# Layer 2's convolution stage of a four-layer kernel: how its strips, loads, stores and token passes are arranged

## The chip, the cores and the metric

The kernel runs on one core of a Trainium2 chip. TensorE (PE in the profile) multiplies matrices, VectorE (DVE), ScalarE (ACT) and GpSimd (POOL) do the element-wise work, and SyncE (SP) issues transfers. A transfer can also be issued from ACT's queue or POOL's. Each engine takes its own instructions strictly in order. The metric is the device time of one execution in microseconds, lower is better.

## The reference

Four layers are chained, each as x = x + layer(groupnorm(x)), on a tensor of 4 images, 384 channels and 64x64 positions in fp32. Layer 0 is an attention, layer 1 a convolution with an 8x8 Fourier filter, layer 3 a 7x7 convolution whose taps depend on the input. The change lies in layer 2, whose core is this:

```python
y3 = _bn(_dw(x, c3_w, 1), c3_g, c3_b)
y5 = _bn(_dw(x, c5_w, 2), c5_g, c5_b)
y1 = x * c1_w.reshape(1, -1, 1, 1) + c1_b.reshape(1, -1, 1, 1)
tok = _bn(kw[:, 0:1] * y3 + kw[:, 1:2] * y5 + y1, ar_g, ar_b)
```

`_dw` is a depthwise convolution (3x3 and 5x5), `_bn` a normalisation of each channel over images and positions, `kw` two weights per image from a small network. After it come a channel gate and a two-matrix network, `cm_w1` (384 to 768) and `cm_w2` (768 to 384).

## The kernel before

The phases run one after the other: `phase_a` (layers 0 and 1), `phase_b` (the convolution stage of layer 2), `phase_ef` (its two matrices), `phase_g` (layer 3). All four are written out as straight code. The framework puts each engine's instructions in an order near that of the program and adds the semaphores.

**Layer 1 of the last image** (image 3) has no attention beside it. It works in 8 bands of 8 rows. `band_out` (L1142) ends each band: two matmuls per output tile, an addition on DVE (L1152), statistics (L630), and a store of the result to DRAM as `x1` from POOL's queue (L1155).

**Strips.** `phase_b` computes the depthwise convolutions as matmuls. Its stationary operand is `z`, a tile of 128 channels in which each channel's image rows are laid out in pairs ("strips", made by TensorE transposes of the normalised x and copied out of PSUM with a scatter). For the first 128 channels, images 0 to 2 are put into `z` by `strips_of` while layer 1 of image 3 runs. Image 3's are made at the head of `phase_b` by `strips5` (L1316): four loads of x1 from DRAM, a normalisation on ACT (L1320), 32 transposes (L1325) and 8 copies to `z` (L1331 on ACT, L1329 on DVE).

**Units.** The 384 channels are worked in 12 units of 32 channels, with all 4 images in the 128 partitions. One unit has 16 steps of two channels each. In a step:

- `matrices53` (L1339) builds the band matrix of the step three steps ahead, from taps loaded on POOL's queue by `taps53` (L1337). Most even steps are built on DVE, odd ones on POOL (L1351).
- `conv53` (L1359) runs 12 matmuls (L1370) into a PSUM bank `conv_m` (4 buffers), two ACT copies into `d_o` (L1379, L1381), two DVE statistics (L1384). Every fourth step stores `d_o` (1 MB) to the DRAM tensor `d53[u]` from ACT's queue (L1386).

Three other streams are threaded through the steps as generators, a piece at a time:

- `unit_strips` (L1261) loads a unit's x1 (two tiles of 1 MB, 8 transfers each, L1272 on SP's queue, into 6 buffers `b_x`), normalises it in four parts (L1280, ACT) and, from unit 4 on, transposes it into `z` (L1294, L1301, L1299). Unit u+1 is processed during unit u.
- `conv_norms` (L1391) turns the finished unit's statistics into factors.
- `unit_tok` (L1427) works on unit u-1 during unit u. For each quarter of 1024 positions it loads 1 MB of convolution results, `c_d` (L1436, SP's queue, 3 buffers), then for each of two halves runs an ACT affine into the single PSUM buffer `tok_m` (L1444) and two DVE operations (L1449, L1451). Then comes an ACT square with a running sum (L1456), and a 512 KB store of the tokens from SP's queue (L1463). The square's output goes to the `c_d` tile, so that tile is free only when the square is done.

After the last unit its own `unit_tok` runs alone, then `tok_stats`, then a short serial chain of small normalisations at the start of `phase_ef`, whose first matmul is L1604. `phase_ef` loads `cm_w2_t` at its beginning, from ACT's queue (L334), although the second matrix is used only half of the phase later (L1658).

Of the kernel before, what the change touches and what calls it, by code (L numbers as in the profile page):

```python
# [281 lines left out]
class _Builder:  # L282
# [859 lines left out]
    def band_out(self, b, acc, h, st):  # L1142

        nc = self.nc
        x = self.block("xa_out", self.xa[b], h, "xo", 2)
        for o in range(NJ):
            m = self.pa("out_m1") if b == B - 1 else self.pm("out_m")
            nc.tensor.matmul(m, lhsT=self.w_out[:, 0, o * P : (o + 1) * P], rhs=acc[1], start=True, stop=False)
            nc.tensor.matmul(
                m, lhsT=self.w_out[64:P, 1, o * P : (o + 1) * P], rhs=acc[2][64:P], start=False, stop=True  # L1150
            )
            nc.vector.tensor_add(x[:, o], x[:, o], m)  # L1152
            yield 2.0
        self.stats(st, x, h)
        nc.gpsimd.dma_start(self.x1[b][:, :, h * 512 : (h + 1) * 512], x)  # L1155


# [3 lines left out]
    def open_strips(self, ctx):  # L1161

        pool = ctx.enter_context(self.tc.tile_pool(name="strips", bufs=1, side="right"))
        self.z_ = pool.tile([P, P * 136 + 4], F32, tag="z", name="z")
        self.z = self.z_[:, 0 : P * 132].rearrange("p (c k b) -> p c k b", k=33, b=B)
        self.nc.gpsimd.memset(self.z[:, :, 0], 0.0)
        self.nc.gpsimd.memset(self.z_[:, P * 132 : P * 132 + 4], 0.0)

    def phase_b(self):
# [5 lines left out]
        with ExitStack() as ctx:  # L1175
# [10 lines left out]
            self.taps53(0)  # L1186
            self.toep = {}
            for n in range(LEAD + 2):
                self.matrices53(n)
            for q in range(4):  # L1190
                x = self.bx_p.tile([P, 2048], F32, tag="x", name="in_x1")[:, 0:1024]
                self.strips5(0, B - 1, x, 8 * q, self.pm)
            self.units(cp)
            self.unit_x = [[] for _ in range(UNITS)]
            strips, behind = self.unit_strips(1), None
            next(strips)
            for u in range(UNITS):
                st = self.bt_p.tile([P, 2, 16, 6], F32, tag="st", name="st")
                tok = self.unit_tok(u - 1) if u else self.unit_strips(0)
                nets = iter(()) if u else self.nets(cp)  # L1200
                for n in range(16):
                    if u or n > 1:
                        self.matrices53(16 * u + n + LEAD)
                    self.conv53(u, n, st)
                    if n == 0 and u:
                        self.conv_norms(u - 1, behind)
                    if n % 2:
                        next(strips, None)
                    elif n or not u:
# [15 lines left out]
            self.tok_stats()  # L1225

# [34 lines left out]
    def unit_strips(self, u):  # L1261
# [22 lines left out]
        load(0)  # L1284
        norm(0)
# [73 lines left out]
    def conv53(self, u, n, st):  # L1359
# [6 lines left out]
        m = self.psum.tile([P, 512], F32, tag="c", name="conv_m", bufs=4)  # L1366
# [59 lines left out]

    def unit_tok(self, u):  # L1427

        nc = self.nc
        j, q = u // 4, u % 4  # L1430
        s, s0 = self.tok_s
        for i in range(4):
            sl = slice(i * 1024, (i + 1) * 1024)
            d = self.bc_p.tile([P, 8, 2, P], F32, tag="d", name="c_d")
            o = self.unit_x[u][i // 2][:, i % 2 * 1024 : i % 2 * 1024 + 1024]
            nc.sync.dma_start(  # L1436
                d.rearrange("p y v n -> p y (v n)"),
                self.d53[u][8 * i : 8 * i + 8].rearrange("y b c v n -> (b c) y (v n)"),
            )
            for h in range(2):  # L1440
                part = slice(h * 512, (h + 1) * 512)
                last = u == UNITS - 1
                m = self.psum.tile([P, 512], F32, tag="c" if last else "t", name="tok_m", bufs=4 if last else 1)
                nc.scalar.activation(  # L1444
                    m, o[:, part], AF.Identity, bias=s0, scale=self.vec("c1_w")[:, u : u + 1]
                )
                mv, ov = (t.rearrange("p (y n) -> p y n", n=P) for t in (m, o[:, part]))
# [6 lines left out]
                if h == 0:  # L1454
                    yield
            nc.scalar.activation(  # L1456
                d.rearrange("p y v n -> p (y v n)")[:, 0:1024],
                o,
                AF.Square,
                bias=self.about[:, u : u + 1],  # L1460
                accum_out=self.squares[:, u, i : i + 1],
            )
            nc.sync.dma_start(self.tok[u, :, :, sl].rearrange("b c n -> (b c) n"), o)  # L1463
            yield
# [59 lines left out]
    def phase_ef(self, strips):  # L1524
        tc, nc = self.tc, self.nc
        with ExitStack() as ctx:
            self.open_psum(ctx)
            cp = ctx.enter_context(tc.tile_pool(name="ef_const", bufs=1))
            w2 = self.weight(cp, "cm_w2_t")
# [50 lines left out]
            for b in range(B):  # L1580
                for i in range(4):
# [18 lines left out]
                    for o in range(6):  # L1600
# [13 lines left out]
                        if o % 2:  # L1614
# [11 lines left out]
                            )  # L1626
                    nc.gpsimd.dma_start(self.wx[b][:, :, blk], x)
# [501 lines left out]
```

## Time and profile before

| what | us |
|---|---|
| median of three runs | 4785.09 |
| the runs | 4772.37, 4785.09, 4792.93 |
| the profiled execution, its own time | 4780.85 |
| its span, first to last instruction | 4779.1 |
| `phase_b`'s first matmul of the convolution | 2452.7 |
| end of its last | 3005.8 |
| first matmul of `phase_ef` (L1604) | 3063.6 |

The page gives, for each engine, the time in which it was busy. Over the whole span that is PE 4377.5 us (92%), DVE 2846.8 (60%), ACT 1964.3 (41%) and POOL 832.4 (17%). Such shares are averages over stages with different limits. To read one stage one asks for the busy time of every engine in stretches of it, with the granted clock of TensorE, the busy share of the 16 transfer engines and the bytes per second. Times in these stretches count from the start of the span.

### The profile page before, as it was taken

The page shows a single profiled execution, that of the slowest core. Times are in us where ns is not written, and L with a number is a line of the kernel's source. Part 1 is how long each engine was busy: PE and PEld are TensorE (multiplying, and loading weights), DVE is VectorE, ACT ScalarE, POOL GpSimd, SP SyncE. Part 2 cuts the span into 40 slices and gives each one's busy share as a digit, 9 for nine tenths or more (in the row PEclk, how much of TensorE's full clock was granted, in tenths as well). Part 3 has the DMA queues.
Part 4 walks back from the last instruction along what each step waited for, and adds up shares of the span by engine and source line. Part 5 has one row for each costly group of instructions (what it writes and reads, how often), then busy time and mean ns, then how long its engine had stood idle before and what let it go on. Part 6 is the DMA issues. An engine that isn't in the chain of part 4 may idle for free. (4 is left out here: it accounts for less than half of the span.)

```text
span 4779.1 us, 49753 instructions
## 1 busy us (share of the span) xinstructions
PE 4377.5 (92%) x18445; PEld 2442.5 (51%) x18445; DVE 2846.8 (60%) x4647; ACT 1964.3 (41%) x2904; POOL 832.4 (17%) x779
## 2 busy tenths in 40 slices
PE   6999999999999999989978899599999999578889
PEld 2233444344443444434457788344444444578889
DVE  7766566645566355565867677655531111777788
ACT  4444444444444443435445566311123332764321
POOL 1000000000000000000035455000000000436665
PEclk9999999999999999999988899799999999688999
DMA  4301211121211111112249789776764333897787
GB/s 144 104 32 65 79 60 67 59 67 38 75 53 62 55 40 60 60 64 97 90 153 308 257 292 305 270 263 251 261 235 178 144 147 131 333 348 235 241 274 259
DMA packets 286592, 747.66 MB, mean 156 GB/s; under 512 B 22555, under 2 KB 123014, under 8 KB 274310
## 3 DMA queue, kind: packets, MB, share of 16 engines
q1 hardware_dynamic: 219832, 442.03, 28.8%
q0 software_dynamic: 40320, 179.59, 10.1%
q10 hardware_dynamic: 26190, 122.76, 6.5%
q8 instruction: 149, 2.44, 0.2%
q14 instruction: 101, 0.83, 0.1%
HBM read 442.04 MB, written 302.25 MB: 156 GB/s over the span
## 5 line engine op out<-in xcount | busy, mean ns | idle before, releaser
L819 ACT ACTIVATE probs<-sc_s 128x1024 f32<-128x1024 f32 x512 | 496.6, 1020 | 688.2 <-PE av L929 588.6
L929 PE MATMUL av<-probs,vt 128*128 128x512 f32 x1536 | 714.9, 602 | 0.0
L1128 DVE SCALAR_TENSOR_TENSOR acc<-band,vecs,acc 128x512 f32<-128x512 f32 x708 | 496.1, 745 | 44.9 <-POOL band L1089 39.7
L1658 PE MATMUL h_m<-f_h,cm_w_t 128*128 128x512 f32 x1152 | 497.1, 594 | 7.4 <-ACT f_h L1646 7.4
L1370 PE MATMUL conv_m<-toep,z 128*128 128x192 f32 (+1 forms) x2304 | 445.8, 355 | 9.2 <-DVE z L1299 9.2
L929 PEld LDWEIGHTS av<-probs,vt 128*128 128x128 f32 x1536 | 275.6, 191 | 338.1 <-issue 334.4
L1987 PE MATMUL conv_m<-toep,z 128*128 128x128 f32 x3072 | 396.4, 287 | 32.5 <-DVE toep L1974 20.6
L1370 PEld LDWEIGHTS conv_m<-toep,z 128*128 128x128 f32 x2304 | 409.6, 197 | 31.9 <-DVE z L1299 9.8
L1987 PEld LDWEIGHTS conv_m<-toep,z 128*128 128x128 f32 x3072 | 382.6, 204 | 34.8 <-issue 13.2
L1604 PE MATMUL h_s<-e_tok,cm_w_t 128*128 128x512 f32 x768 | 362.8, 595 | 4.2 <-DVE e_tok L1589 4.2
L1658 PEld LDWEIGHTS h_m<-f_h,cm_w_t 128*128 128x128 f32 x1152 | 219.7, 191 | 284.8 <-issue 274.7
L1666 DVE BATCH_NORM_STATS2 h_st<-f_h 128x6 f32<-128x512 f32 x96 | 66.4, 693 | 429.6 <-ACT f_h L1665 429.6
L811 PE MATMUL sc_s<-q,k 32*128 32x512 f32 x2048 | 306.6, 642 | 14.9 <-ACT probs L819 14.7
L1351 POOL TENSOR_TENSOR toep<-w,band 128x1280 f32<-128x1280 f32 x94 | 272.3, 2897 | 240.0 <-PE conv_m L1370 236.8
L1051 PE MATMUL t_m<-w_in_t,xb 128*128 128x384 f32 x768 | 279.2, 498 | 4.2 <-DVE coef L1068 4.0
L965 PE MATMUL proj_m<-xm,w_proj_t 128*128 128x512 f32 x576 | 271.8, 611 | 6.3 <-DVE xm L904 4.9
L1611 ACT COPY e_h<-h_s 128x1024 f32<-128x1024 f32 x96 | 97.2, 1013 | 399.6 <-PE h_s L1604 395.5
L1613 DVE BATCH_NORM_STATS2 h_st<-e_h 128x6 f32<-128x512 f32 x192 | 123.5, 685 | 207.9 <-ACT e_h L1611 207.9
L1604 PEld LDWEIGHTS h_s<-e_tok,cm_w_t 128*128 128x128 f32 x768 | 146.3, 191 | 188.0 <-issue 183.2
L1051 PEld LDWEIGHTS t_m<-w_in_t,xb 128*128 128x128 f32 x768 | 143.0, 192 | 142.1 <-issue 60.0
L972 DVE SCALAR_TENSOR_TENSOR x_res<-proj_m,bn_c,x_res 128x512 f32<-128x512 f32 x96 | 71.7, 747 | 236.4 <-PE proj_m L965 236.3
L1604 PE MATMUL h_s<-z,cm_w_t 128*128 128x512 f32 x384 | 196.1, 592 | 0.0
(426 smaller groups left out, 6371.6 us busy)
## 6 DMA issues: line engine op xcount, KB each, us to landing
d<-d_o ACTq DMA_DIRECT2D x48, 1024.0 KB
c_d<-d SPq DMA_DIRECT2D x48, 1024.0 KB
hid<-e_h ACTq DMA_DIRECT2D x16, 3072.0 KB
f_h<-hid SPq DMA_DIRECT2D x16, 3072.0 KB
x_in<-in_x SPq DMA_DIRECT2D x96, 256.0 KB
x_res<-in_x SPq DMA_DIRECT2D x32, 768.0 KB
xa<-x_res POOLq DMA_DIRECT2D x32, 768.0 KB, 3.9
xa_out<-xa SPq DMA_DIRECT2D x32, 768.0 KB
```

The costliest lines, as they stand in the source:

```text
L811: nc.tensor.matmul(s[:, g], lhsT=k4[32 * g : 32 * g + 32, c], rhs=q[i][32 * g : 32 * g + 32], start=True, stop=True,)
L819: nc.scalar.activation(p[:, h * 1024 : (h + 1) * 1024], s[:, 2 * h : 2 * h + 2].rearrange("p a b -> p (a b)"), AF.Exp, scale=0.25,)
L929: nc.tensor.matmul(av[0], lhsT=vt[:, 4 * c + v, :], rhs=p[:, v * 512 : (v + 1) * 512], start=c == 0 and v == 0, stop=c == 7 and v == 3,)
L965: nc.tensor.matmul(m, lhsT=self.w_proj[:, j, o * P : (o + 1) * P], rhs=xm[:, j], start=j == 0, stop=j == NJ - 1,)
L1051: nc.tensor.matmul(m[:, 0:C], lhsT=xb[:, j], rhs=self.w_in[:, j, :], start=j == 0, stop=j == NJ - 1,)
L1128: nc.vector.scalar_tensor_tensor(out, src(j, k), w, done, ALU.mult, ALU.add)
L1351: eng.tensor_tensor(t, self.w53[:, at : at + 160].rearrange("p (m n) -> p m n", n=8).unsqueeze(2).to_broadcast([P, 20, 8, 8]), band.rearra ...
L1370: nc.tensor.matmul(m[:, c * 256 + to : c * 256 + to + 64 * (k1 - k0)], lhsT=self.z_[:, at : at + P], rhs=t[:, 10 * c + k0 : 10 * c + k1].r ...
L1604: nc.tensor.matmul(s[:, v, :], lhsT=w1[:, j, o * P : (o + 1) * P], rhs=t[j][:, v * 512 : (v + 1) * 512], start=j == 0, stop=j == NJ - 1,)
L1613: nc.vector.bn_stats(st[:, o, 8 * b + 2 * i + v, :], h[:, o, v * 512 : (v + 1) * 512])
L1658: nc.tensor.matmul(m, lhsT=w2[:, o, j * P : (j + 1) * P], rhs=h[:, o, v * 512 : (v + 1) * 512], start=o == 0, stop=o == 5,)
L1987: nc.tensor.matmul(m[:, ch % 4 * P : (ch % 4 + 1) * P], lhsT=self.z_[:, at : at + P], rhs=t[:, 8 * c + 2 * i : 8 * c + 2 * i + 2].rearrang ...
```

## The change

In the order of the program:

1. Image 3's strips of the first 128 channels are transposed, not normalised, at the end of each band of layer 1 (`raw_strips`). At the head of `phase_b` the factors of the group norm are spread over the partitions (`strip_factors`, one matmul), and `z` is scaled in place (`scale_strips`): 8 channels on DVE, then 24 on DVE, then three times 32 on POOL at steps 3, 7 and 11 of unit 0. The loads, normalisations, transposes and copies of `strips5` for that image go.
2. The first taps are loaded when the strips' pool is opened, into a pool of their own with 2 buffers (3 before).
3. `units` and `nets` move behind the first convolution step. A unit's first x tile is asked for at step 11, and no longer at step 15, of two units earlier, and a `yield` parts that load from its normalisation.
4. The results of a finished unit are asked for at step 0 of the next (three tiles), and the fourth when the first tile's square is done. The last unit's four tiles use the `b_x` buffers.
5. `tok_m` has 2 buffers and `conv_m` 3. The square of a quarter, and its store, follow behind the next quarter's first affine (`square_and_store`), and the store is issued from ACT's queue. In the last unit, the tokens of the unit before are taken in larger portions.
6. `cm_w2_t` is loaded from POOL's queue after the second block of `phase_ef`.

```diff
@@ -1151,9 +1151,37 @@
+        if b == B - 1:
+            self.raw_strips(b, h, x[:, 0])
         self.stats(st, x, h)
...
+    def raw_strips(self, b, h, x):
+
+        m = self.pm("strip_m")
+        for k in range(4):
+            self.nc.tensor.transpose(m[:, k * P : (k + 1) * P], x[:, k * P : (k + 1) * P], self.ident)
+        self.nc.scalar.copy(self.z[:, :, 1 + 4 * h : 5 + 4 * h, b], m.rearrange("p (k c) -> p c k", c=P))
+
+    def strip_factors(self, b):
+
+        nc = self.nc
+        x = self.bx_p.tile([P, 2048], F32, tag="x", name="z_rep")
+        t, self.z_rep = (x[:, 256 * i : 256 * i + 256].rearrange("p (i c) -> p i c", i=2) for i in range(2))
+        for i, v in enumerate((self.r2, self.n2)):
+            nc.vector.tensor_scalar(t[:, i], self.ident, v[:, 0, b : b + 1], float(P), ALU.mult, ALU.mult)
+        m = self.pm("z_rep")[:, 0 : 2 * P]
+        nc.tensor.matmul(m, lhsT=self.mean128, rhs=t.rearrange("p i c -> p (i c)"), start=True, stop=True)
+        nc.vector.tensor_copy(self.z_rep, m.rearrange("p (i c) -> p i c", i=2))
+
+    def scale_strips(self, b, c0, n, eng):
+
+        at = slice(c0, c0 + n)
+        zv = self.z[:, at, 1:33, b]
+        of = lambda i: self.z_rep[:, i, at].unsqueeze(2).to_broadcast([P, n, 32])
+        eng.tensor_mul(zv, zv, of(0))
+        eng.tensor_add(zv, zv, of(1))
@@ -1165,6 +1193,9 @@
+        self.taps_s = ExitStack()
+        self.taps_p = self.taps_s.enter_context(self.tc.tile_pool(name="b_taps", bufs=2, side="right"))
+        self.taps53(0)
@@ -1183,46 +1214,62 @@
-            self.taps53(0)
             for n in range(LEAD + 2):
+                if n == 1:
+                    self.strip_factors(B - 1)
+                    self.scale_strips(B - 1, 0, 8, nc.vector)
+                if n == 3:
+                    self.scale_strips(B - 1, 8, 24, nc.vector)
                 self.matrices53(n)
-            for q in range(4):
-                x = self.bx_p.tile([P, 2048], F32, tag="x", name="in_x1")[:, 0:1024]
-                self.strips5(0, B - 1, x, 8 * q, self.pm)
-            self.units(cp)
             self.unit_x = [[] for _ in range(UNITS)]
-            strips, behind = self.unit_strips(1), None
-            next(strips)
+            first, strips, behind = self.unit_strips(0), self.unit_strips(1), None
+            next(first)
             for u in range(UNITS):
                 st = self.bt_p.tile([P, 2, 16, 6], F32, tag="st", name="st")
-                tok = self.unit_tok(u - 1) if u else self.unit_strips(0)
-                nets = iter(()) if u else self.nets(cp)
                 for n in range(16):
                     self.conv53(u, n, st)
+                    if n == 0 and not u:
+                        self.units(cp)
+                        nets = self.nets(cp)
+                        for _ in range(2):
+                            next(first)
+                    if n == 0 and u > 1:
+                        next(before, None)
                     if n == 0 and u:
+                        self.results = [self.load_results(u - 1, i) for i in range(3)]
                         self.conv_norms(u - 1, behind)
+                    if not u and n in (3, 7, 11):
+                        self.scale_strips(B - 1, 8 * n + 8, 32, nc.gpsimd)
                     if n % 2:
                         next(strips, None)
                     elif n or not u:
                         next(tok, None)
-                    if n == 15 and u:
+                    if u == UNITS - 1 and n or u and n == 15:
                         next(tok, None)
+                    if not u and n in (1, 3):
+                        next(strips)
...
                     if n % 3 == 2:
                         next(nets, None)
-                    if n == 15 and u + 2 < UNITS:
-                        strips = self.unit_strips(u + 2)
-                        next(strips)
-                behind = st
+                    if n in (11, 15) and u + 2 < UNITS:
+                        if n == 11:
+                            coming = self.unit_strips(u + 2)
+                        next(coming)
+                        if n == 15:
+                            strips = coming
+                behind, before = st, tok
+            self.results = [self.load_results(UNITS - 1, i, self.bx_p, "x") for i in range(4)]
             self.conv_norms(UNITS - 1, behind)
             for _ in self.unit_tok(UNITS - 1):
                 pass
             self.tok_stats()
+        self.taps_s.close()
@@ -1282,6 +1329,7 @@
             )
 
         load(0)
+        yield
         norm(0)
         yield
-            self.w53_ahead = self.bt_p.tile([P, 8 * 80], F32, tag="w53", name="w53", bufs=3)
+            self.w53_ahead = self.taps_p.tile([P, 8 * 80], F32, tag="w53", name="w53", bufs=2)
-        m = self.psum.tile([P, 512], F32, tag="c", name="conv_m", bufs=4)
+        m = self.psum.tile([P, 512], F32, tag="c", name="conv_m", bufs=3)
+    def load_results(self, u, i, pool=None, tag="d"):
+        pool = pool or self.bc_p
+        d = pool.tile([P, 2 * 8 * P], F32, tag=tag, name="c_d").rearrange("p (y v n) -> p y v n", v=2, n=P)
+        self.nc.sync.dma_start(
+            d.rearrange("p y v n -> p y (v n)"),
+            self.d53[u][8 * i : 8 * i + 8].rearrange("y b c v n -> (b c) y (v n)"),
+        )
+        return d
+
...
+        results, self.results = self.results, None
+        behind = None
         for i in range(4):
-            sl = slice(i * 1024, (i + 1) * 1024)
-            d = self.bc_p.tile([P, 8, 2, P], F32, tag="d", name="c_d")
+            d = results[i]
             o = self.unit_x[u][i // 2][:, i % 2 * 1024 : i % 2 * 1024 + 1024]
-            nc.sync.dma_start(
-                d.rearrange("p y v n -> p y (v n)"),
-                self.d53[u][8 * i : 8 * i + 8].rearrange("y b c v n -> (b c) y (v n)"),
-            )
             for h in range(2):
                 part = slice(h * 512, (h + 1) * 512)
-                last = u == UNITS - 1
-                m = self.psum.tile([P, 512], F32, tag="c" if last else "t", name="tok_m", bufs=4 if last else 1)
+                m = self.psum.tile([P, 512], F32, tag="t", name="tok_m", bufs=2)
                 nc.scalar.activation(
                     m, o[:, part], AF.Identity, bias=s0, scale=self.vec("c1_w")[:, u : u + 1]
                 )
+                if h == 0 and behind is not None:
+                    self.square_and_store(u, *behind)
+                    if len(results) == 3:
+                        results.append(self.load_results(u, 3))
                 mv, ov = (t.rearrange("p (y n) -> p y n", n=P) for t in (m, o[:, part]))
                 of = lambda v: d[:, 4 * h : 4 * h + 4, v]
                 nc.vector.scalar_tensor_tensor(mv, of(1), s[:, 1:2], mv, ALU.mult, ALU.add)
-                if h == 0:
-                    yield
...
-            nc.sync.dma_start(self.tok[u, :, :, sl].rearrange("b c n -> (b c) n"), o)
-            yield
+                yield
+            behind = i, d, o
+        self.square_and_store(u, *behind)
...
+    def square_and_store(self, u, i, d, o):
...
+        nc.scalar.dma_start(self.tok[u, :, :, i * 1024 : i * 1024 + 1024].rearrange("b c n -> (b c) n"), o)
@@ -1526,7 +1586,7 @@
-            w2 = self.weight(cp, "cm_w2_t")
+            w2 = cp.tile(list(self.ins["cm_w2_t"].shape), F32, tag="cm_w2_t", name="cm_w2_t")
...
+                    if b == 0 and i == 1:
+                        nc.gpsimd.dma_start(w2, self.ins["cm_w2_t"])
```

More of the change, by code (lines that the diff above doesn't have):

```diff
@@ L1185, in phase_b @@
             nc.gpsimd.memset(self.mean128, 1.0 / P)
-            self.taps53(0)
             self.toep = {}
             for n in range(LEAD + 2):
+                if n == 1:
[3 more added lines that the diff above has]
+                    self.scale_strips(B - 1, 8, 24, nc.vector)
                 self.matrices53(n)
-            for q in range(4):
-                x = self.bx_p.tile([P, 2048], F32, tag="x", name="in_x1")[:, 0:1024]
-                self.strips5(0, B - 1, x, 8 * q, self.pm)
-            self.units(cp)
             self.unit_x = [[] for _ in range(UNITS)]
-            strips, behind = self.unit_strips(1), None
-            next(strips)
+            first, strips, behind = self.unit_strips(0), self.unit_strips(1), None
+            next(first)
             for u in range(UNITS):
                 st = self.bt_p.tile([P, 2, 16, 6], F32, tag="st", name="st")
-                tok = self.unit_tok(u - 1) if u else self.unit_strips(0)
-                nets = iter(()) if u else self.nets(cp)
+                tok = self.unit_tok(u - 1) if u else first
                 for n in range(16):
@@ L1425, in conv_norms @@
         self.tok_s = s, s0
+    def load_results(self, u, i, pool=None, tag="d"):
[6 more added lines that the diff above has]
+        return d
     def unit_tok(self, u):
         nc = self.nc
-        j, q = u // 4, u % 4
         s, s0 = self.tok_s
+        results, self.results = self.results, None
+        behind = None
         for i in range(4):
-            sl = slice(i * 1024, (i + 1) * 1024)
-            d = self.bc_p.tile([P, 8, 2, P], F32, tag="d", name="c_d")
+            d = results[i]
             o = self.unit_x[u][i // 2][:, i % 2 * 1024 : i % 2 * 1024 + 1024]
-            nc.sync.dma_start(
-                d.rearrange("p y v n -> p y (v n)"),
-                self.d53[u][8 * i : 8 * i + 8].rearrange("y b c v n -> (b c) y (v n)"),
-            )
             for h in range(2):
                 part = slice(h * 512, (h + 1) * 512)
-                last = u == UNITS - 1
-                m = self.psum.tile([P, 512], F32, tag="c" if last else "t", name="tok_m", bufs=4 if last else 1)
+                m = self.psum.tile([P, 512], F32, tag="t", name="tok_m", bufs=2)
                 nc.scalar.activation(
@@ L1453, in unit_tok @@
                 )
-                if h == 0:
-                    yield
[L1456 to L1463, printed above, removed]
-            yield
+                yield
+            behind = i, d, o
+        self.square_and_store(u, *behind)
+    def square_and_store(self, u, i, d, o):
+        nc = self.nc
+        nc.scalar.activation(
+            d.rearrange("p y v n -> p (y v n)")[:, 0:1024],
+            o,
+            AF.Square,
+            bias=self.about[:, u : u + 1],
+            accum_out=self.squares[:, u, i : i + 1],
+        )
+        nc.scalar.dma_start(self.tok[u, :, :, i * 1024 : i * 1024 + 1024].rearrange("b c n -> (b c) n"), o)
     def tok_stats(self):
```

## The prediction

> **What bounds the kernel now.** The slices of the page only say that transfers are busiest in the middle of the span, so I cut the convolution stage into stretches, at the first matmul of each unit. The columns are length, busy time of PE, PEld, DVE, ACT and POOL, granted clock, transfer share, GB/s. In order: the head, units 0, 2 and 3, units 7 to 10 together, unit 11, and the tail up to the first matmul of `phase_ef`.
>
> ```profile
> core 0: us, PE busy (x) PEld busy (x) DVE busy (x) ACT busy (x) POOL busy (x), PEclk, DMA share, GB/s
> 2431.00:2452.70 21.70, 9.20 (x35) 6.39 (x35) 12.91 (x22) 9.60 (x10) 2.19 (x4) 0.50 0.95 272
> 2452.70:2490.60 37.90, 37.88 (x204) 35.22 (x205) 27.39 (x62) 24.44 (x51) 23.91 (x11) 0.95 0.46 154
> 2527.90:2563.60 35.70, 35.70 (x204) 34.05 (x203) 33.48 (x70) 20.38 (x50) 25.54 (x13) 1.00 0.91 326
> 2563.60:2632.80 69.20, 44.42 (x238) 40.72 (x236) 44.84 (x92) 40.70 (x80) 27.11 (x14) 0.78 0.95 308
> 2779.80:2966.00 186.20, 168.78 (x936) 157.27 (x937) 145.08 (x290) 115.28 (x247) 102.20 (x48) 0.94 0.90 300
> 2966.00:3005.80 39.80, 39.80 (x201) 37.67 (x201) 30.27 (x68) 21.43 (x50) 17.40 (x6) 0.89 0.86 300
> 3005.80:3063.60 57.80, 5.83 (x28) 4.61 (x26) 28.91 (x96) 25.86 (x46) 0.00 (x0) 0.53 0.86 279
> ```
>
> A unit without strips takes PE 35.7 us, one with them 42.2 (168.78 / 4), and then PE idles 4.4. Unit 3 idles 25. Transfers are never far from full. So two things lie close together, PE and the transfers, and the losses come where they get out of step. What holds the loads back is in the waits of SP's queue over the same stage, named as waiting line, releaser, us, times, longest:
>
> ```profile
> SPq L1463 <- DVE st L1384: 165.1, 30, 12.6
> SPq L1272 <- DMA d<-d_o: 65.6, 11, 19.4
> SPq L1463 <- DVE unit_x L1451: 48.8, 9, 16.1
> SPq L1272 <- DMA tok<-unit_x: 45.1, 18, 6.2
> SPq L1463 <- DVE cn_s L1424: 16.3, 2, 14.3
> SPq L1436 <- DMA d<-d_o: 29.4, 8, 8.1
> ```
>
> L1463 is the token store. It stands at the head of the queue until DVE has produced the tokens, 237 us in all (165.1 + 48.8 + 16.3, and 7.1 in a line not shown), and every later load stands behind it. The chain of waits shows what that does to unit 9 (start, duration, what):
>
> ```profile
> 2897.63 1.30 SPq L1272
> 2898.97 6.08 DMA unit_x<-x
> 2905.08 1.25 ACT unit_x L1280
> 2906.38 1.09 PE strip_m L1294 x8
> ...
> 2918.23 1.11 PE strip_m L1294 x8
> 2919.36 1.07 DVE z L1299
> 2920.47 0.69 PE cn_rep L1402 x2
> ```
>
> The load of the second x tile is issued halfway through the unit, so its strips end the unit and the next one waits for them. In the tail the same chain shows the serial path:
>
> ```profile
> 3006.88 9.03 DMA d<-d_o
> ...
> 3018.00 12.16 DMA c_d<-d
> ...
> 3039.02 5.95 DMA z<-tok
> ```
>
> **The change, part by part.** The sum is made against the profiled execution, 4780.85 us.
>
> **Layer 1's end.** Added: 8 times 4 transposes and one copy. Eight transposes took 1.09 us of PE at full clock (chain above), so four take 0.55, and eight bands 4.4 us. The copy to `z` has a row of the same scatter: L1331, 1.08 us, so 8.7 us of ACT, which was busy 102 of 180 us there (2180 to 2360) and has room. PE was busy 174 of those 180, so the transposes of about six bands lie on the path: 3.3 us. Each also holds one of two PSUM buffers until ACT copies it, some 2 us in which the Fourier matmuls have one buffer. I put that at 1.7 us in all. The later two bands are set by DVE. **+5**, from 0 (all in gaps) to +12 (1.5 us per band). Should PE have gaps that I don't see, nothing is lost.
>
> **Head.** Gone: 4 loads of 512 KB, 4 ACT normalisations (1.24), 32 transposes, 8 copies (1.07). They fill the time from the norm's last operation (2432.6) to the first convolution (2452.7). Left before that convolution: one band matrix (1.48, the mean of L1351), two small DVE operations (about 0.3 each, between the 0.31 of the 128x144 L1254 and the 0.23 of L1183), a 256-column matmul at the half clock that this stretch shows (about 1.2, from 0.85 for L1252's two passes of 144 columns), one PSUM copy (0.4, L1407), two DVE operations on 256 elements (0.3 each, from 1.48 us per 1280): 4.3 us, or 4.6 with the steps between engines, so 2437. The taps, waited for until 2439.1 before, are there already. **-15** (-11 with a late band matrix, -17 without any gap). Then DVE scales 24 channels (2 x 0.9) between matrices, under the slow first steps. `units` moves behind step 0, where its 0.85 us matmul costs under 1 us of PE.
>
> **Unit 0.** POOL gets 6 operations on 1024 elements. L1974 has this shape on POOL, 2.4 us: 14.5 us on top of 23.9 in 37.9. It is just full, and its band matrices come a little late: 39 in place of 37.9. The next channels are needed only a unit later.
>
> **The order of loads and stores.** 48 stores of 0.34 us leave SP and go to ACT's queue (0.33 as in L1386): 4 per unit, 1.3 us, into 17 us of ACT idle time per unit (28.8 of 46.6 busy). They are issued behind the square, when their data is long ready, so ACT doesn't wait for DVE there. The rest of the ACT queue, `d_o`'s copies above all, moves up. Two rows of waits shrink: the ACT affine on its single PSUM buffer (44.3 us), the square on DVE (39.0). They are no PE time in themselves.
>
> Here the Trainium skill speaks against the change. In "DMA: Bandwidth & Descriptors", section "Issuing engines are not separate DMA queues", it says that all issuing engines share the same 16 transfer engines and a second one only saves issue time. By that rule the move is worth 48 x 0.34 = 16 us of a queue that nobody waits for, hence 0, and the whole sum below is -27: 4754 on the profile. By the row, SP stands 237 us with loads behind it. Both hold: no bandwidth is won, but order is. I go by the row, as the transfer share falls to 0.73 in unit 4 and 0.75 in unit 6 (lines not shown) while PE idles.
>
> How much? A unit moves 13.9 MB: x 2.1, `d` out 4.2 and back 4.2, tokens 2.1, taps 1.3. Units 1 to 11 moved 148 MB (515.2 us at 288 GB/s), and will move some 150, with less left for the tail. At the 300 GB/s of units 7 to 10 they need 500 us, at the 326 of unit 2, the best, 460. I take 315, between them: 476, and with unit 0 515 us in place of 553.1. By units: 39 + 2 x 38.5 + 8 x 45 + 39. PE alone would need 37 + 2 x 36 + 8 x 42.2 + 38 = 485. **-38**, from 0 to -68. What is late next: the three `c_d` loads now wait at the head of SP's queue for the last `d` store, and the second x tile stands behind them.
>
> The third `conv_m` buffer: PE can still run two steps (4.4 us) ahead of ACT, and ACT's longest waits are among those that go. 0. Two tap buffers: a load (6.6 us to landing, 9.5 at worst) is needed four steps, some 9 us, later, as before. 0, and a 1 us wait at worst if POOL is behind.
>
> **Tail.** From 3005.8 the tokens of unit 10 are still being worked, stores and `cm_w2_t` share the engines, and the last token operation ends at 3047. Unit 10's tokens will be done, and four buffers are free at once: `d` store 1.1 us to issue and some 5 to land (3.9 was the best, 9.0 here), 4.2 MB at 340 GB/s 12.3 and 2 of latency, the last pair of DVE operations 3: 23.5 in place of 41.2. The 16.6 us of small operations behind stay. **-17** (-8 if loads land no sooner, -22). `cm_w2_t` goes into the next stage, where PE is busy 579 of 586 us and the transfer share is 0.66; its first use is at 3567. 0.
>
> **Sum:** +5 - 15 - 38 - 17 = -65, so 4716 for the profiled execution. That lies 4 us under the median of the runs, so for the median **4720**.
>
> **Rivals.**
>
> - **PE sets the stage** (0.17). Everything is on time and the floor of 485 is reached: -68 in place of -38, 4690. For it: unit 2 ran at 35.70 of 35.70. Against: 150 MB would have to go at 335 GB/s for 446 us.
> - **The transfers set it** (0.18). Units 7 to 10 already show a share of 0.90. Then 39 + 500: -14, and 4744. Against: their own idle steps are explained by the order.
> - **Slower: the second x tile comes late** (0.08). In SP's queue it now follows three 1 MB loads that wait for the last `d` store (9 us after the unit starts). Single `c_d` loads took 6.7 to 10.2 us in the chain. If they follow each other at 8 us and the x tile too, it lands 41 us into the unit. Its ACT normalisation at step 7 (18 us) blocks the copies behind it, and PE. In such an order 17 us are lost in eight units: 42.2 + 17 against 50.3 now is +71, with the ends' -27 a time of 4829. It decides from a stall of 11.5 us per unit (8.1 + 27 / 8). Against: loads that overlap share a rate of 300 GB/s, which brings all four in 14 us.
> - **Little happens** (0.07). The transposes cost 12, the head gives 11, the tail 8, and the stage stays at 553: 4778, within the noise.
> - The forecast has 0.50, with a range of its own of 4695 to 4746.
>
> **How the numbers follow.** Half a per cent, 24 us, is about what a measurement of this kernel can tell from no change. Faster by more is the forecast and the first two rivals: 0.85. Slower 0.08, the same 0.07. The range from 4677 to 4773 holds the forecast and most of the first two rivals (0.80), and leaves out the slow rival, "little happens" and some of the fastest.
>
> **What would show it.** Right: the first convolution 4 to 5 us behind the norm's last operation, where it is 20 now; no wait of SP on the token store; units 3 to 10 at 43 to 47 us with unit 3 no longer at 69; a tail near 40 us. Wrong: ACT waiting long for x tiles or SP for `d` stores (the slow rival), a transfer share above 0.95 with PE idle (the transfer rival), or a last stage of layer 1 longer by over 10 us.

## The result and the profile after

The changed kernel takes **4739.55 us** (median of 5 runs, 4732.08 to 4751.16) against 4785.09 before: a ratio of 0.9908, with a 95% interval of 0.9884 to 0.9933. It is faster by 0.9%; 4720 had been predicted, with 4677 to 4773 as the range. The profiled execution took 4751.16 us, the longest of the five: its instructions ahead of the last image's layer 1, which the change doesn't touch, end 10 us later than in the profile before. Among the profiles of all kernels here the last matmul of that part (L929) starts between 2132.5 and 2145.3 us, whichever edit they carry, so lengths of stages are compared, not absolute times.

Stretches of the kernel after, with the columns of the prediction's first view: head, units 0, 2 and 3, units 7 to 10 together, unit 11, the tail.

```profile
2454.10:2467.80 13.70, 1.98 (x10) 1.40 (x10) 13.61 (x16) 0.00 (x0) 8.98 (x4) 0.50 0.73 173
2467.80:2511.40 43.60, 40.63 (x199) 37.69 (x200) 35.52 (x61) 24.47 (x51) 32.55 (x15) 0.88 0.42 142
2558.50:2600.50 42.00, 37.71 (x204) 34.78 (x204) 33.13 (x67) 24.62 (x55) 25.56 (x12) 0.98 0.96 319
2600.50:2646.70 46.20, 41.81 (x235) 38.56 (x234) 38.08 (x80) 30.63 (x68) 25.55 (x12) 0.96 0.96 330
2774.10:2941.90 167.80, 158.95 (x936) 149.21 (x937) 144.22 (x293) 114.57 (x249) 102.29 (x48) 1.00 0.98 333
2941.90:2982.20 40.30, 37.85 (x202) 35.55 (x202) 33.05 (x74) 21.75 (x52) 17.96 (x7) 0.96 0.81 296
2982.20:3028.40 46.20, 4.68 (x25) 3.72 (x24) 24.12 (x81) 19.51 (x36) 0.80 (x1) 0.55 0.96 317
```

Units 7 to 10 take 42.0 us each (46.6 before) with transfers at 0.98. Unit 3 has lost its hole (46.2 for 69.2 before). But units 0 and 2 got slower (37.9 and 35.7 before), unit 0 with transfers at only 0.42. The waits of SP's queue have no line of the token store any more:

```profile
SPq L1319 <- DMA tok<-unit_x: 90.0, 11, 10.9
SPq L1478 <- DMA d<-d_o: 77.4, 12, 13.9
SPq L1319 <- DMA c_d<-d: 76.6, 12, 10.5
SPq L1319 <- DMA d<-d_o: 51.8, 7, 27.3
```

SP now waits for transfers (L1319 loads x, L1478 the convolution's results), not for DVE. In the head, the timeline shows what stands between the norm's last operation (L1028) and the first convolution (L1418):

```profile
2454.04 0.16 DVE L1028 COPY norm<-gn_n 128x3 f32<-128x3 f32 x1
...
2454.94 1.49 DVE L1399 TENSOR_TENSOR toep<-w,band_p 128x1280 f32<-128x1280 f32 x1
...
2456.73 1.48 DVE L1399 TENSOR_TENSOR toep<-w,band_p 128x1280 f32<-128x1280 f32 x1
...
2458.60 1.48 DVE L1399 TENSOR_TENSOR toep<-w,band_p 128x1280 f32<-128x1280 f32 x1
2458.82 4.96 POOL L1183 TENSOR_TENSOR z<-z,z_rep 128x1024 f32<-128x1024 f32 x2 [8.87 <-DVE z_rep L1176]
2459.99 5.19 DVE L1183 TENSOR_TENSOR z<-z,z_rep 128x256 f32<-128x256 f32 x2
2463.74 6.13 POOL L1184 TENSOR_TENSOR z<-z,z_rep 128x1024 f32<-128x1024 f32 x2
2464.99 6.31 DVE L1184 TENSOR_TENSOR z<-z,z_rep 128x256 f32<-128x256 f32 x2
```

DVE scales 8 channels (128x256) and 24 (128x768): singly 1.68 and 3.66 us for the products (L1183), 2.76 and 3.72 for the sums (L1184). POOL's scaling, written behind step 3 of unit 0, was pulled ahead by the planner (the part of the framework that orders each engine's instructions), and runs beside them.

In the tail, the chain of waits still has a load of the results as its longest step:

```profile
2982.96 3.87 DMA d<-d_o
...
2992.25 14.13 DMA c_d<-d
```

Stage by stage, from the first operation of layer 1's last image to the end: layer 1 257.8 us before and 269.9 after; from the norm to the first convolution 20.0 and 13.6; the convolution section 553.1 and 514.4; tail 57.4 and 46.2; everything behind 1715.5 and 1720.6. The first four differ by -44, all five by -39, and the medians by -45.5. Cut in two, the section shows where its 39 us come from (units 0 to 3, then 4 to 11; first before, then after):

```profile
2452.70:2632.80 180.10, 154.01 (x844) 143.99 (x844) 132.15 (x277) 104.32 (x223) 102.03 (x48) 0.91 0.80 268
2632.80:3005.80 373.00, 336.54 (x1837) 313.84 (x1838) 281.71 (x573) 221.15 (x480) 196.16 (x90) 0.93 0.86 285
```

```profile
2467.80:2646.70 178.90, 160.17 (x836) 148.35 (x837) 142.76 (x284) 105.54 (x227) 110.68 (x52) 0.93 0.79 268
2646.70:2982.20 335.50, 316.15 (x1840) 296.64 (x1840) 285.58 (x585) 221.69 (x487) 196.87 (x91) 0.99 0.96 328
```

All but 1 us of it is in units 4 to 11, where the transfer share rises from 0.86 to 0.96. In the first part two changes cancel: unit 3 is 23 us shorter, and units 0 to 2 together are 22 us longer.

### The profile page after: what moved, and what is told of

It is laid out like the page before. It is cut to its first block, busy times and chain, and to the rows that moved or that the text cites. A ratio compares the mean times of both kernels' runs of the same rounds, so it can differ in the third digit from the quotient of the medians.

```text
span 4749.0 us, 49714 instructions
## 1 busy us (share of the span) xinstructions
PE 4376.2 (92%) x18447; PEld 2434.2 (51%) x18447; DVE 2851.0 (60%) x4650; ACT 1958.1 (41%) x2904; POOL 845.5 (18%) x786
## 3 DMA queue, kind: packets, MB, share of 16 engines
q0 software_dynamic: 40464, 180.77, 10.1%
## 5 line engine op out<-in xcount | busy, mean ns | idle before, releaser
L929 PE MATMUL av<-probs,vt 128*128 128x512 f32 x1536 | 721.8, 607 | 0.0
L1418 PE MATMUL conv_m<-toep,z 128*128 128x192 f32 (+1 forms) x2304 | 446.9, 352 | 33.3 <-DVE z L1347 12.5
L929 PEld LDWEIGHTS av<-probs,vt 128*128 128x128 f32 x1536 | 278.0, 192 | 342.3 <-issue 338.6
L1418 PEld LDWEIGHTS conv_m<-toep,z 128*128 128x128 f32 x2304 | 403.3, 195 | 56.8 <-ACT d_o L1429 16.9
L1399 POOL TENSOR_TENSOR toep<-w,band 128x1280 f32<-128x1280 f32 x94 | 272.5, 2899 | 179.2 <-PE conv_m L1418 179.2
```

Of the source, the lines that this page charges most:

```text
L929: nc.tensor.matmul(av[0], lhsT=vt[:, 4 * c + v, :], rhs=p[:, v * 512 : (v + 1) * 512], start=c == 0 and v == 0, stop=c == 7 and v == 3,)
L1399: eng.tensor_tensor(t, self.w53[:, at : at + 160].rearrange("p (m n) -> p m n", n=8).unsqueeze(2).to_broadcast([P, 20, 8, 8]), band.rearra ...
L1418: nc.tensor.matmul(m[:, c * 256 + to : c * 256 + to + 64 * (k1 - k0)], lhsT=self.z_[:, at : at + P], rhs=t[:, 10 * c + k0 : 10 * c + k1].r ...
```

## The experiments

The table holds what the profiles show from the last image's layer 1 on, one profile for each kernel. The head runs from the norm's last operation to the first convolution, the section is units 0 to 11 together, and the tail runs from the last convolution to the first matmul of `phase_ef`. Beside each length is the time that transfers were busy in it (their share times the length). "First token" is the issue of the first token store, from the first convolution on. Times in us.

| kernel | layer 1 | head | units 0-3 (transfers) | units 4-11 (transfers) | tail | first token | median |
|---|---|---|---|---|---|---|---|
| before | 257.8 | 20.0 | 180.1 (145) | 373.0 (319) | 57.4 | 83 | 4785.1 |
| after | 269.9 | 13.6 | 178.9 (141) | 335.5 (322) | 46.2 | 77 | 4739.6 |
| e1_store_sp | 269.8 | 13.6 | 186.0 (150) | 362.9 (324) | 43.9 | 83 | 4763.9 |
| e2_no_raw | 259.9 | 15.7 | 165.4 (141) | 333.4 (317) | 46.7 | 65 | 4716.7 |
| e3_factors_psum | 267.8 | 9.8 | 182.5 (144) | 331.1 (321) | 46.1 | 83 | 4733.6 |
| e4_late_loads | 267.4 | 13.6 | 188.1 (147) | 351.1 (326) | 46.6 | 90 | 4763.3 |
| e5_scale_dve | 268.0 | 5.6 | 181.6 (148) | 334.8 (318) | 45.7 | 81 | 4737.9 |
| e6_raw_only | 267.9 | 13.5 | 181.2 (144) | 375.2 (317) | 53.3 | 85 | 4791.1 |
| e7_w2_early | 260.6 | 15.7 | 167.9 (143) | 330.4 (319) | 52.7 | 67 | 4721.9 |
| e9_scale_later | 269.7 | 5.6 | 197.3 (149) | 332.1 (318) | 46.0 | 87 | 4746.0 |
| e10_whole_tiles | 259.7 | 14.3 | 168.0 (147) | 336.2 (323) | 47.3 | 70 | 4728.7 |
| e11_psum41 | 260.2 | 15.7 | 171.6 (144) | 348.9 (319) | 61.5 | 73 | 4749.0 |
| e12_early_x | 259.7 | 15.7 | 174.9 (146) | 331.9 (319) | 45.9 | 75 | 4718.3 |

Two things to read from it. Transfers are busy for 141 to 150 us in the first column and 317 to 326 in the second, whatever the order: no bandwidth is won or lost, only idle time. And the planner places every instruction anew, so an edit moves more than its own line. The earlier x tile, the tap buffers and the larger portions in the last unit were not undone by themselves.

**The store back on SP's queue.**

```
-        nc.scalar.dma_start(self.tok[u, :, :, ...
+        nc.sync.dma_start(self.tok[u, :, :, ...
```

> The kernel after, with one thing undone: the token store is issued from SP's queue again. Order theory (the move of the store is what shortened the convolution section): SP waits on DVE's tokens again, 100 us or more in all at the store's line, and the x loads behind it start late; the section goes from 514 us back to between 530 and 553, the whole kernel 16 to 39 us up, 4755 to 4778. Rival, after the rule that a second issuing queue saves issue time only: the section stays at 514 within 3 us, because the early loads and the earlier x tile carry the gain; 4737 to 4742.

The section went to 548.9 us and the kernel to 4763.9 (0.9949 of before, 0.9928 to 0.9969): the order theory, and about half of the change's whole gain. Not as expected were the waits: SP stood only some 50 us at the store's own line (L1524), and longer at the loads (168.2 and 122.6 us, where the kernel after has 77.4 and 51.8). So the run shows what the move is worth, and leaves open through which of these waits.

```profile
SPq L1478 <- DMA d<-d_o: 168.2, 17, 13.7
SPq L1319 <- DMA d<-d_o: 122.6, 15, 27.4
SPq L1319 <- DMA c_d<-d: 32.7, 12, 4.5
SPq L1524 <- DVE st L1432: 26.1, 13, 5.1
```

An x load has no use for `d`. In the program, transfers issued by SP and ACT take turns on eight completion semaphores, and each waits for the one that had its semaphore before it; so a load can wait for a `d` store issued on ACT. That the two queues are tied in this way is read from the program; how much of the 122.6 us it costs was not measured by itself.

**The loads of the results late again.**

```
-    self.results = [self.load_results(u - 1, i) for i in range(3)]
...
-            d = results[i]
+            d = self.load_results(u, i)
```

> The kernel after, where each load of convolution results is issued again where its tokens are worked, and not three at a time at the unit's start; the store stays on ACT's queue. Theory (the store is what blocked): the section stays within 6 us of 514, the tail of 46 us grows by 4 to 10 because the last loads wait in line again; 4743 to 4756. Rival (the early loads carry the gain): the section goes up to 530 or more, SP or DVE waiting for results in each unit; 4760 or more.

The section went to 539.2 us, the kernel to 4763.3: the rival. So the early loads carry about as much of the kernel's time as the store's move. Undone one by one, the two give back 34.5 and 24.8 us of the section, 59.3 in sum, of a gain of 38.7: they are not two separate gains, and at least 20 us need both.

**The PSUM buffers as before**, on the kernel without raw strips (below).

```
-        m = self.psum.tile([P, 512], F32, tag="c", name="conv_m", bufs=3)
+        m = self.psum.tile([P, 512], F32, tag="c", name="conv_m", bufs=4)
...
-                m = self.psum.tile([P, 512], F32, tag="t", name="tok_m", bufs=2)
+                m = self.psum.tile([P, 512], F32, tag="t", name="tok_m", bufs=1)
```

> The kernel without raw strips, with the PSUM buffers of the stage as before: four for the convolution's sums, one for the tokens. Theory (the prediction's: the split is worth nothing): section 499 within 4 us, 4713 to 4721. Rival (the second token buffer is what lets ACT run ahead, and carries part of the 38 us): the section at 507 or more, ACT's affine waiting on DVE for 20 us or more in all, 4725 or more.

The rival, and clearly: 4749.0 us, 32 slower than with two token buffers. The edit also gives the convolution its fourth buffer back, which nothing here shows to cost time, so the loss is put to the token buffer. ACT's affine on one buffer (waits of ACT's queue in the stage, first with one, then with two):

```profile
ACT tok_m L1496 <- DVE unit_x L1507: 129.9, 63, 5.2
```

```profile
ACT tok_m L1496 <- DVE unit_x L1507: 5.4, 4, 3.7
```

While ACT waits there, its queue's copies and stores wait too: 15 us more in units 4 to 11, 6 in units 0 to 3, and 15 in the tail. (Before the change the tail had four buffers of its own, so only the first two sums say what the split is worth.)

**Without raw strips.**

```
-        if b == B - 1:
-            self.raw_strips(b, h, x[:, 0])
...
+            for q in range(4):
+                x = self.bx_p.tile(...)[:, 0:1024]
+                self.strips5(0, B - 1, x, 8 * q, self.pm)
```

> The kernel after without the raw strips: layer 1's end as it was, and the head loads, normalises and turns the last image's strips as before. Theory (the raw strips cost about 12 us in layer 1 and give 6 in the head): layer 1's last stage is 257 us again in place of 269, the way from the norm's last operation to the first convolution 20 us in place of 13.8, the convolution section 514 as after; in sum 6 us less, about 4733. Rival (layer 1 is longer for another reason, such as the tap buffers that now lie on the other side of the memory, or from one execution to the next): the stage stays near 269, and the kernel comes out 6 us slower, about 4746.

**4716.7 us, 0.9862 of before (0.9841 to 0.9883): the fastest version found**, by 23 us against the kernel after. Layer 1 gave 10 us, as the theory had it, and the head took back only 2. But units 0 to 3 came down by 13.5, which neither theory had. The head without raw strips is 15.7, not 20, probably because the taps, which the first matrices waited for, are loaded in layer 1 now.

**Raw strips alone, on the kernel before.** The same functions and calls, with the order and buffers of before.

> The kernel before, with the raw strips alone: transposes in layer 1, scaling in the head and in unit 0; its order of loads and stores, buffers and queues as before. Theory (what the runs so far show: 10 us more in layer 1, 6 less in the head, and up to 15 more in units 0 to 2): 4 to 19 us slower than before, 4789 to 4803. Rival (the terms of the prediction, +5 and -15): 10 us faster than before, 4775.

0.2% slower than before (1.0018, 1.0006 to 1.003): layer 1 +10.1, head -6.5, units 0 to 3 +1. The prediction's terms for layer 1 and the head, -10 in sum, were wrong in sign. In layer 1 PE is busy for 243.1 us in place of 236.0 (windows over the stage, before and with raw strips; PE first, with its count):

```profile
2169.70:2427.50 257.80, 236.04 (x766) 117.35 (x764) 185.37 (x284) 121.91 (x217) 13.87 (x24) 0.95 0.27 90
```

```profile
2173.60:2441.50 267.90, 243.08 (x798) 121.20 (x796) 185.48 (x284) 128.66 (x224) 10.78 (x24) 0.95 0.27 87
```

So PE is busy 7.0 us longer, where the transposes were priced at 4.4, and idle 3.1 us longer.

**DVE's factors from PSUM.**

```
-        m = self.pm("z_rep")[:, 0 : 2 * P]
+        m = self.rep_p          # columns 256 to 511 of the band's PSUM tile
...
-        of = lambda i: self.z_rep[...]
+        of = lambda i: (self.rep_p if eng is self.nc.vector else self.z_rep)[...]
```

> The kernel after, where DVE takes the scaling's factors from PSUM and not from SBUF, so that its two operations have one SBUF input each; POOL's scaling is unchanged and runs beside it. Theory (DVE and POOL hold each other up when both read two inputs from SBUF): DVE's 128x256 operations take 0.3 to 0.5 us in place of 1.7 and 2.8, the 128x768 ones 0.9 to 1.1 in place of 3.7; the first convolution starts 6 to 8 us behind the norm's last operation in place of 13.8, and the kernel is 6 us shorter, about 4733. Rival (the scattered layout of the strips, 16 bytes from element to element, is what is slow): the four durations stay within 10%, and so does the time.

Theory right, with sizes of its own: 0.61 and 0.60 us in place of 1.68 and 2.76, 1.59 and 1.62 in place of 3.66 and 3.72, with POOL scaling beside them at 2.38 to 2.46 an operation (2.38 to 3.63 in the kernel after). In these rows DVE, with two inputs in SBUF, is held until POOL's operation ends. The clearest rows are two tiny operations that were left with two SBUF inputs (12 elements per partition, and one):

```profile
2448.09 4.73 POOL L1183 TENSOR_TENSOR z<-z,z_rep 128x1024 f32<-128x1024 f32 x2 [8.78 <-DMA unit_x<-x]
2448.38 2.11 DVE L1284 TENSOR_TENSOR c_u<-norm_u,vecs 128x12 f32<-128x12 f32 x1
2450.41 2.41 DVE L383 TENSOR_TENSOR net_a<-net_a,vecs 12x1 f32<-12x1 f32 x1
```

They end at 2450.49 and 2452.82, and so do POOL's two operations, within 0.05 us. The first takes 0.17 us without raw strips, where POOL scales nothing. The head came down to 9.8, and these two are 4.5 of it. The kernel's 4733.6 is within the noise of 4739.6.

**All scaling on DVE**, and **POOL's scaling later**, both with the factors in PSUM.

```
-                        self.scale_strips(B - 1, 8 * n + 8, 32, nc.gpsimd)
+                        self.scale_strips(B - 1, 8 * n + 8, 32, nc.vector)
```

> The kernel after, with all of the scaling on DVE, its factors in PSUM; POOL scales nothing. The run without raw strips had units 0 to 2 in 118 us, the kernel after in 133. Theory (POOL's six scaling operations, some 15 us, delay its band matrices and hold DVE up in unit 0): units 0 to 2 come down to 118 to 124 us, the section to 500 to 506, and the first convolution starts 7 to 9 us after the norm; the kernel at 4720 to 4730. Rival (the transfers or the slow first steps of a cold TensorE cost it): units 0 to 2 stay at 128 to 135, the section at 512 or more, 4731 to 4740; DVE takes some 13 us more in unit 0 and could be late itself.

```
-                    if not u and n in (3, 7, 11):
-                        self.scale_strips(B - 1, 8 * n + 8, 32, nc.gpsimd)
+                    if 16 * u + n in (9, 17, 31):
+                        with self.tc.issue_after(self.last[True].ins): self.scale_strips(...)
```

> The kernel after, with DVE's factors in PSUM, and POOL's three pairs of scaling operations no longer run beside the head: the first pair is put behind a band matrix in the middle of unit 0, the second at the start of unit 1, the third at its end. Theory (the 15 us that the section loses with raw strips come from scaling and small DVE operations meeting in the head and unit 0: PE stalls there and restarts at half clock): units 0 to 2 come from 133 us to 118 to 124, the section to 500 to 506, the first convolution 6 to 8 us behind the norm; 4720 to 4727. Rival (it is the later start of the transfers, or DVE's own load in unit 0): units 0 to 2 stay at 128 us or more, the section above 510, 4731 or more.

Both theories fell. The head is 5.6 us in both, close to the 4.6 of the prediction, yet units 0 to 3 stayed at 181.6 and grew to 197.3. A faster head is worth nothing that these runs can tell. What did follow the length of units 0 to 3 is the first token store: in twelve of the thirteen kernels they end 96 to 103 us after it (110 with POOL's scaling later). That is a relation, not a proof of cause.

**Both x tiles of unit 2 early**, without raw strips.

```
-                    if n in (11, 15) and u + 2 < UNITS:
+                    if n in (11 if u else 3, 15) and u + 2 < UNITS:
...
-        load(0)
+        load(0); u == 2 and load(1)
```

> The kernel without raw strips, with both x tiles of unit 2 loaded at step 3 of unit 0, 2.1 MB that would else move in units 0's end and 1. Theory (from unit 1 on the transfers set the pace at some 335 GB/s, so what moves in unit 0, where their share is 0.54, is gained): the section gets 4 to 7 us shorter, unit 3 43 us or less in place of 47.3; 4710 to 4714. Rival (the pace is set unit by unit by the way x load, strips, tokens, store; the early tiles only wait): the section stays within 2 us of 499, 4715 to 4719.

Neither: units 0 to 3 got 9.5 us longer, and unit 0 moved hardly more (6.6 MB for 6.4). The early loads stood in SP's queue ahead of unit 0's results, whose first load went out 61.6 us after the first convolution in place of 45.6, and the first token store 10 us later.

**Whole tiles.** Four loads of 256 KB for a tile in place of eight of 128 KB, without raw strips.

> The kernel without raw strips, with each x tile loaded by four transfers of 256 KB in place of eight of 128 KB; same bytes. In the program, transfers issued by SP and ACT take turns on eight completion semaphores, and each waits for the one that had its semaphore before, so an x load can wait for a d store on ACT's queue that it has nothing to do with (48.5 us of SP's waits without raw strips, 46.5 in the first two units of the kernel after alone). Theory (that is what leaves transfers idle for 24 us in units 0 to 3): with half the x loads these waits fall below 30 us, units 0 to 3 come from 165 us to 155 or less, the kernel to 4700 to 4710. Rival (the idle time of the first units is the lack of data to move, whatever the semaphores): units 0 to 3 stay within 4 us of 165, 4713 to 4720; or whole tiles land later, and it is slower.

The rival, or a little worse: SP's x loads waited 45.6 us for `d` stores in the first two units (38.3 with eight loads a tile), not under 30, and units 0 to 3 took 168.0. So the number of loads is not it, and what an x load's wait on a `d` store costs stays open.

**The next stage's weight early**, without raw strips: `cm_w2_t` loaded at the start of `phase_ef`, as before the change.

> The kernel without raw strips, where the load of the next stage's second weight is issued at that stage's beginning again. Theory (part of the shorter tail comes from keeping that load out of it): the tail goes from 46.7 us to 50 or more, about the 3.5 us of 1.2 MB at 340 GB/s, and the kernel to 4720 or more. Rival (the tail is a chain of latencies, and a load beside it costs nothing): the tail stays within 1.5 us, the time within 3.

The tail took 52.7 us, the theory, though the kernel's 4721.9 overlaps with 4716.7.

**Less PE work**, without raw strips: one of three matmuls, that of the three leading taps, is left out, so the kernel computes less than the reference asks. It ran once.

```
-            for i, k0, k1, to in ((1, 3, 7, 0), (0, 0, 3, 0), (2, 7, 10, 64)):
+            for i, k0, k1, to in ((1, 3, 7, 0), (2, 7, 10, 64)):
```

> The kernel without raw strips, with one of the three matmuls of every channel left out of layer 2's convolution (that of the three leading taps), 32 of 192 columns in each unit, about 6 us of PE; this leaves out part of the computation. Theory (PE sets the pace of units 4 to 10, 41.7 us each with PE busy for 39.7): these units come down to 36 or 37 us. Rival (the transfers set it, 13.9 MB at 330 to 340 GB/s in each): they stay at 40.5 to 42, and PE idles for 7 us in each.

Units 4 to 10 of this kernel, and then of the one that it was made from:

```profile
2622.90:2925.50 302.60, 237.33 (x1190) 208.92 (x1190) 252.83 (x512) 196.99 (x434) 178.58 (x84) 0.90 0.96 324
```

```profile
2615.80:2909.00 293.20, 278.40 (x1638) 261.05 (x1638) 252.30 (x512) 200.03 (x435) 178.89 (x84) 1.00 0.97 333
```

PE lost 41 us of work in these seven units, and they took no less: 43.2 and 41.9 us each, with transfers at 0.96 and 0.97. In the new order **the transfers set the pace of units 4 to 10**, and PE is the one that waits, though with all its work it is close behind (39.8 of 41.9 us).

## Why the prediction was right, and where it was not

The direction and the place were right: most of it is the order of loads and stores. The size came out at -44 in the four stages of the sum, which said -65, and the raw strips, counted as a gain of 10, cost 23 us: the change gains in spite of them. Two of the signs named for being wrong came too: layer 1 grew by over 10 us, and in units 7 to 10 transfers are at 0.98 with PE idle, the sign of the transfer rival, though at a better rate than that rival gave them. Term by term:

- **The order, -38.** Measured -38.7, at 514.4 us for 515. But this is luck, as two errors cancel. By its own units the prediction had 161 us for units 0 to 3 and 354 for 4 to 11; they took 179 and 336. The rate was mis-sized: 315 GB/s was taken, between two rows, and units 4 to 11 ran at 328 with transfers at 0.96, so this part went the way of the transfer rival, at the best rate seen before, not its 300 GB/s. Unit 0's 39 us took 43.6, units 1 and 2 took 89.1 for 77: of the gain expected in units 0 to 3, 1 us came.
- **By the rule or by the row.** The rule of "DMA: Bandwidth & Descriptors" made the store's move worth 0, the row made it -38 in sum with the early loads. With the move alone undone the section lost 34.5 us. What the rule says of bandwidth holds here (transfers are busy for the same time within 7% in all kernels of the table). What it leaves out is that an issue which waits holds up what stands behind it: SP stood 237 us at the token store before. With the store put back it stood there for only some 50, so the path of the 34.5 us is not this wait alone.
- **The PSUM split, 0: the step that failed.** I priced only what the third convolution buffer loses, and took the two rows of ACT's waits (44.3 and 39.0 us) for "no PE time in themselves". Without the second token buffer ACT waits 129.9 us for DVE where it waits 5.4 with it, and the section is 22 us longer (520.6 against 498.8).
- **Layer 1, +5.** Measured +12.1 here, +10 in the kernel before with raw strips alone: the term was mis-sized, and lies at the end of its bounds. PE's added work was 7.0 us for 4.4 and its added idle time 3.1 for the 1.7 of waiting; which bands lie on the path was not measured. Some 2 us of the 12.1 are not of the strips, as layer 1 takes 259.9 without them.
- **Head, -15.** Measured -6.4. DVE's two first operations were priced at 0.3 each from the band matrix's row. That row has its factor in PSUM; the new ones have both inputs in SBUF and took 1.68 and 2.76, with the 24 channels' product (3.66) placed between them. And three band matrices of 1.5 us (L1399) stood ahead of them, where one was counted. The rows of a held operation were in the trace of before: there L383, one element per partition, takes 1.75 us from 2462.40 and ends at 2464.15 with POOL's band matrix (2461.25, 2.89).

```profile
2461.25 2.89 POOL L1351 TENSOR_TENSOR toep<-w,band 128x1280 f32<-128x1280 f32 x1 [1.43 <-DVE st L1384]
2462.40 1.75 DVE L383 TENSOR_TENSOR net_a<-net_a,vecs 12x1 f32<-12x1 f32 x1
```

  The Trainium skill says so in "GPSIMD Engine Reference", section "Specifications": GpSimd's interfaces to SBUF are shared with VectorE, and an instruction of VectorE with two SBUF inputs contends. By the page the head would not have been priced from a row with one; the runs put the price at the rest of POOL's operation. Even so the head isn't where it matters.
- **Tail, -17.** Measured -11.2. The `d` store and the loads' landing took no longer than they were given (3.9 and 14.1 us), but the last token operation ended 29.2 us behind the convolution, not 23.5: the four loads needed 5.4 us to go out (2986.9 to 2992.3), which the sum left out, and the last pair of operations 5, not 3. Keeping `cm_w2_t` out of the tail, priced at 0 by itself, was worth 6 us of it in the run that undid that.
- **The slower rival** (a late second x tile) showed nowhere: PE idles 2.0 to 4.1 us in each of units 4 to 11, where it decides from 11.5.

What units 0 to 3 lose with raw strips is settled in part: PE's time in unit 0 and the first token store come later, and in units 4 to 11 the transfers, at 0.96, have little idle time left to make it up. That this is the reason is argued, not shown. Which of the planner's placements causes the loss stays open; moving the scaling off POOL or later did not cure it.

## What to carry to other kernels

Where a store waits for its data at the head of the queue that issues the loads, try it on another queue, even where all transfers share the same engines. Here that paid in full only with the loads issued early and a second token buffer, so undo such parts one at a time before crediting any. Before a step is moved onto an idle engine, look for its neighbours' operands: here, on DVE, two inputs in SBUF beside a busy POOL cost the rest of POOL's operation. And where transfers are full for most of a stage, its start can decide: count how long they idle in the first units.

## What was not expected of the hardware

A short hole in PE's work cost nearly as much again in clock. In unit 0 of the kernel after, one DVE operation on 12 partitions (L384, 0.15 us in the kernel before) took 3.45 us and ended at 2482.28, with POOL's band matrix. ACT waited 3.74 us for what follows from it, its copies out of PSUM came late, and PE idled 2.88 us:

```profile
2478.83 3.45 DVE L384 TENSOR_TENSOR net_c<-net_mv,net_a 12x1 f32<-12x1 f32 x1
2479.36 2.91 POOL L1399 TENSOR_TENSOR toep<-w,band 128x1280 f32<-128x1280 f32 x1
...
2482.50 0.35 ACT L412 ACTIVATE net_h<-net_z,net_c,net_a 12x4 f32<-12x4 f32 x1 [3.74 <-DVE net_c L385]
```

The stretches before, in and behind the hole:

```profile
2480.00:2483.10 3.10, 3.01 (x19) 2.51 (x17) 3.06 (x3) 0.58 (x2) 2.80 (x2) 1.00 0.36 106
2483.10:2485.98 2.88, 0.00 (x0) 0.00 (x0) 1.08 (x2) 2.87 (x5) 2.86 (x2) 0.84 0.44 121
2485.98:2491.40 5.42, 5.42 (x15) 4.88 (x16) 3.66 (x10) 3.23 (x9) 0.78 (x2) 0.50 0.55 222
```

The granted clock fell to 0.50, and was there for all of the 5.42 us behind the hole: 2.7 us of work lost behind 2.9 us of waiting. The Trainium skill, in "TensorE: Matmul & The Clock Gate", section "HAM oscillation — how this bites in real kernels", warns of gaps above some 3.4 us; in this one place a shorter one was enough, and the measurement decides.
